# Moving five early loads from SyncE's queue to GpSimd's, behind the weights, and nine warm-up products in place of fourteen

## The chip, the cores and the metric

The kernel runs on one core of a Trainium2 chip. The metric is the device time of one execution in microseconds (us), taken as the median of several runs. Engines are named as in the profile: PE is TensorE's matmul side and PEld its weight loads, DVE is VectorE, ACT is ScalarE, POOL is GpSimd, SP is SyncE. L267 is line 267 of the kernel file before the change.

## The reference, cut to what matters

The input x has 4 sequences of 1024 rows and 256 columns, in 32-bit floats. Three residual steps follow each other:

```
def tlin(x, w, s): return einsum('bsi,oi->bso', x, w) * s      # w holds -1, 0, 1

def ffn(x):
    h = silu(tlin(x, w1, s1)) * tlin(x, w2, s2)    # 256 -> 1024
    h = gelu(tlin(h, h1, t1))                      # 1024 -> 1024
    h = gelu(tlin(h, h2, t2))                      # 1024 -> 1024
    return tlin(h, w3, s3)                         # 1024 -> 256

x = x + 0.5 * ffn(layernorm(x))
x = x + mix(layernorm(x))      # long convolution by FFT with a computed kernel, gelu, then @ W.T + b
x = x + 0.5 * ffn(layernorm(x))
```

Both feed-forward steps use the same weights. `w3s` holds s3, `wt` holds W transposed and `bias` holds b.

## The kernel before

The 4096 rows are cut into eight blocks of 512. The list of work is eight blocks of the first feed-forward step (turn "f", blocks 0 to 7), then eight of the last (turn "g"). The mixing step and the computation of its convolution kernel are Python generators that are advanced by small steps (`tick`) among the matmuls of the blocks.

For one block, `transposed` turns the normalized rows into two tiles `xt` by eight PE transposes, and `ffn` runs four layers. In the first, for each of eight groups m of 128 outputs, `linear` (L267) makes `pa` from w1 and `pb` from w2. Each takes four matmuls, since there are two groups k of inputs and each activation is held in two parts of reduced width. ACT applies the silu (L286), DVE multiplies (L287), ACT makes the first part of the result `ha` (L289) and DVE the second (L240). The layers with `h1` and `h2` take 16 matmuls for each m. The output layer (L323) uses w3, and `finish` (L332) scales by `w3s_sb`.

All weights stay on chip. They are loaded at the start in one queue, `weights_from`, which is POOL's in the form of the kernel that runs: w1 and w2 in two pieces each (256 narrow columns, then the 768 wide ones, L191 and L192), then the rows of block 1, the inputs of the convolution kernel (`k_in`), h1 and h2 in eight pieces (L201), and w3 (L202). The two halves of block 0's rows are issued by SP and ACT (L182). SP then issues small constants, `w3s_sb`, `wt_sb` and `bias_sb` (L203 to L205), and after them the rows of blocks 2 and 3 (L171, called by `load_x`). The buffers of the rows (tag "xb") are three, so that the rows of block 3 wait for block 0's buffer, which comes free when block 0 is transposed.

Ahead of block 0, PE multiplies an identity by itself N_WARM times (L880). A 32-bit product of this kind shows in the profile as two matmul instructions.

The order of the instructions on each engine is not the order of the program text. A planner orders them when the program is built, by their place in the text as a priority and by times that it expects for transfers and operations. On the chip each engine runs its own list strictly in that order: an instruction that waits holds up all behind it. Tiles of one tag share a fixed number of buffers (19 of tag "half", 15 of tag "ring", 8 PSUM banks).

`prepare` loads and normalizes the next block while the current one is computed; in the text its steps for block 2 come in the last wide layer of block 1, but the planner may place them as early as the buffer allows.

Of the kernel before, what the change touches and what calls it, by code (L numbers as in the profile page):

```python
# [17 lines left out]
P = 128  # L18
# [10 lines left out]
NA, NB = 64, 16  # L29
A0, A1 = 8, 8  # L30
JQ = J // 2
N_WARM = 14
STEPS = 2 * KH - 1
N_CHECKS = 44

# [58 lines left out]
def macaron_layers(  # L94
# [23 lines left out]
    nc = tc.nc  # L118
# [10 lines left out]
    def bank(name):  # L129
        return psum.tile([P, 512], F32, tag="ps", name=name)  # L130
# [20 lines left out]
    wt_sb = keep.tile([P, DC, D], F32, name="wt_sb")  # L151
    w3s_sb = keep.tile([P, D], F32, name="w3s_sb")
    bias_sb = keep.tile([P, D], F32, name="bias_sb")
# [11 lines left out]
    def positions(t, b, j, n=2):  # L165
        return t[b].rearrange("(p j) d -> p j d", j=J)[:, j : j + n, :]

    def load_x(t, blk, name, queue=nc.sync):
        b, g = divmod(blk, J // JT)
        xb = work.tile([P, JT, D], F32, tag="xb", name=name, bufs=3)  # L170
        queue.dma_start(xb, positions(t, b, g * JT, JT))  # L171
        return xb

    def rows(w):
        return w.rearrange("(k p) o -> p k o", p=P)


    weights_from = nc.gpsimd if split else nc.sync
# [15 lines left out]
    x_second = load_x(x, 1, "x_f1", queue=weights_from)  # L194
# [5 lines left out]
        for k in range(0, KH, 2):  # L200
            weights_from.dma_start(t[:, k : k + 2, :], rows(src)[:, k : k + 2, :])  # L201
    weights_from.dma_start(w3_sb, rows(w3))  # L202
    nc.sync.dma_start(w3s_sb, w3_s.partition_broadcast(P))  # L203
    nc.sync.dma_start(wt_sb, rows(wt))
    nc.sync.dma_start(bias_sb, bias.partition_broadcast(P))  # L205


    def norm(t, name, parts_of=1):

        stats = small.tile([P, JT, 6], F32, tag="stats", name=f"stats_{name}")  # L210
        mv = small.tile([P, JT, 2], F32, tag="mv", name=f"mv_{name}")
        rstd = small.tile([P, JT], F32, tag="rstd", name=f"rstd_{name}")
        step = JT // parts_of
        for at in range(0, JT, step):
            here = range(at, at + step)
            for i in here:
                nc.vector.bn_stats(stats[:, i, :], t[:, i, :])
            for i in here:
                nc.vector.bn_aggr(mv[:, i, :], stats[:, i, :])
            nc.scalar.activation(  # L220
                rstd[:, at : at + step], mv[:, at : at + step, 1], AF.Sqrt, bias=eps
            )
        yield
        for at in range(0, JT, step):
            nc.vector.reciprocal(rstd[:, at : at + step], rstd[:, at : at + step])
            for i in range(at, at + step):
                ts(
                    t[:, i, :],
                    t[:, i, :],
                    mv[:, i, 0:1],  # L230
                    rstd[:, i : i + 1],
                    ALU.subtract,
                    ALU.mult,
                )
        yield
# [6 lines left out]
    def transposed(xn, name, first=False):  # L242


        pts = [bank(f"pt_{name}_{k}") for k in range(DC)]
        order = [(k, i) for k in range(DC) for i in range(JT)]
        for k, i in sorted(order, key=lambda o: o[1]) if first else order:
            nc.tensor.transpose(  # L248
                pts[k][:, i * P : (i + 1) * P], xn[:, i, k * P : (k + 1) * P], ident
            )  # L250
        xt = [ring(f"xt_{name}_{k}", parts, TB, dtype=wide) for k in range(DC)]
        last = None
        if first:
            last = nc.vector.tensor_copy(xt[0][:, 0, :], pts[0])
            nc.scalar.copy(xt[1][:, 0, :], pts[1])
        for k in range(DC):
            if not first:
                nc.vector.tensor_copy(xt[k][:, 0, :], pts[k])
            if split:
                last = low_part(xt[k], pts[k])  # L260
        return (xt, last) if first else xt
# [572 lines left out]
    def prepare(turn, blk, upcoming):  # L834

        name = f"{turn}{blk}"
        if turn == "f":
            xb = x_second if blk == 1 else load_x(x, blk, f"x_{name}")
        else:
            while ("m", blk // 2) not in done:  # L840
                next(aside, None)
            xb = load_x(x2, blk, f"x_{name}")
        yield
        yield
        for _ in norm(xb, name):
            yield
            yield
        while True:
            if ("last layer", blk, turn) in done:
                upcoming.extend(transposed(xb, name))  # L850
                return
            yield
# [25 lines left out]
    warm = bank("warm")  # L878
    for i in range(N_WARM):
        nc.tensor.matmul(warm[:, 0:P], ident, ident, start=(i == 0), stop=(i == N_WARM - 1))  # L880
    for _ in norm(x_first, "f0", parts_of=2):
        pass
    xt, last_split = transposed(x_first, "f0", first=True)
    for n, (turn, blk) in enumerate(blocks):
        following = []
        steps = [prepare(*b, following) for b in blocks[n + 1 : n + 2]]

        def ahead(last=False):
            for step in steps:
                if last:  # L890
                    done.append(("last layer", *blocks[n + 1][::-1]))
                next(step, None)

        src, dst = (x, x1) if turn == "f" else (x2, out)
        with tc.issue_after(last_split.ins) if n == 0 else nullcontext():
            ffn(xt, src, dst, blk, f"{turn}{blk}", tick, ahead, n + 1 == len(blocks))
        done.append((turn, blk))
        xt = following
# [5 lines left out]
def macaron_kernel(tc: tile.TileContext, *args):  # L904
    nc = tc.nc
    with tc.tile_pool(name="flag", bufs=1) as flags:
        bad = flags.tile([1, 1], I32, name="bad")
        macaron_layers(tc, bad, *args)
        n_bad = nc.values_load(bad, min_val=0, max_val=1 << 24)
        with tc.If(n_bad > 0):  # L910
            macaron_layers(tc, None, *args)
# [65 lines left out]
```

## Time and profile before

| What | Value |
|---|---|
| Median of three runs | 1436.28 us (1435.95 to 1436.58) |
| Profiled execution: its own time | 1436.93 us |
| Profiled execution: span from first to last instruction | 1435.2 us |
| PE busy | 1420.1 us, 99% of the span |
| PEld busy | 1203.3 us, 84% |
| DVE busy | 834.3 us, 58% |
| ACT busy | 674.2 us, 47% |
| POOL busy | 79.1 us, 6% |
| Bytes moved | 85.50 MB, 60 GB/s over the span |
| Bytes moved in the first 40 us | 362 GB/s |

The page has a row for each engine with its busy time, and a strip that cuts the span into 40 slices. The transfers are dense in the first slice alone; the matmuls are dense in all but the first and last. Queue q0 in the profile is POOL's, q1 is SP's and q10 is ACT's. A timeline row gives the start, the time from the start of the first to the end of the last of a merged group, the engine and line, the operation, the output and inputs by name, the count and, in brackets, the idle time ahead of it with what ended it. Matmuls overlap, so that the distance between the starts of two, rather than the duration of one, is what PE spends on each.

### The profile page before, as it was taken

How to read it: one execution, taken by the hardware profiler on the slowest of the kernel's cores; microseconds unless marked ns; L12 is line 12 of the kernel's file. 1: busy time of each engine (PE TensorE's matmuls, PEld its weight loads, DVE VectorE, ACT ScalarE, POOL GpSimd, SP SyncE). 2: the span in 40 equal slices, each digit the busy share in tenths (PEclk: the TensorE clock that was granted, in tenths of full speed). 3: DMA queues.
4: the chain of work that ended last, by engine and by line, in shares of the span. 5: the costliest groups of instructions: out<-in, count | busy, mean ns of one | idle time of the engine just before them, and what ended most of it. 6: DMA issues, size and time to landing. Idle time of an engine off the chain costs nothing.

```text
span 1435.2 us, 18151 instructions
## 1 busy us (share of the span) xinstructions
PE 1420.1 (99%) x7102; PEld 1203.3 (84%) x7102; DVE 834.3 (58%) x1584; ACT 674.2 (47%) x1030; POOL 79.1 (6%) x77
## 2 busy tenths in 40 slices
PE   7999999999999999999999999999999999999998
PEld 6888888888888888888888888888888888888886
DVE  5786566853745587653787722966547766341422
ACT  4776458744534345334553433534344344443432
POOL 3010000100000000020000010000010000100000
PEclk9999999999999999999999999999999999999999
DMA  9110000101132130140131130231131311300000
GB/s 366 40 45 0 16 30 0 45 1 30 56 111 69 38 125 30 59 127 21 46 109 39 65 111 22 88 96 37 60 103 52 91 42 37 96 30 1 23 8 18
DMA packets 43662, 85.50 MB, mean 60 GB/s; under 512 B 4832, under 2 KB 10720, under 8 KB 43568
## 3 DMA queue, kind: packets, MB, share of 16 engines
q1 hardware_dynamic: 38864, 71.62, 15.5%
q0 software_dynamic: 4560, 12.39, 2.4%
q8 instruction: 57, 0.93, 0.3%
q14 instruction: 37, 0.30, 0.1%
q10 hardware_dynamic: 144, 0.26, 0.0%
HBM read 69.04 MB, written 15.20 MB: 59 GB/s over the span
## 4 chain that ended last, share of the span: by engine, by line
PE 97%; DVE 1%; DMA 1%; POOL 0%; issue 0%; POOLq 0%
PE p_g L267 32%; PE p_f L267 31%; PE po_g L323 4%; PE po_f L323 4%; PE pb_f L267 4%; PE pa_f L267 4%; PE pa_g L267 4%; PE pb_g L267 4%; PE pi L791 2%; PE pw L811 2%; PE pf_m L621 2%; PE pk L552 1%; DMA w_sb<-in_w_dram 1%; PE pf_k L621 0%; PE pt_g L248 0%; PE pt_f L248 0%
## 5 line engine op out<-in xcount | busy, mean ns | idle before, releaser
L267 PE MATMUL p_f<-h_f,h_sb 128*128 128x512 f32 x1024 | 239.1, 392 | 0.0
L267 PE MATMUL p_f<-ha_f,h_sb 128*128 128x512 f32 x1024 | 237.0, 391 | 0.0
L267 PE MATMUL p_g<-h_g,h_sb 128*128 128x512 f32 x1024 | 236.0, 390 | 0.0
L267 PE MATMUL p_g<-ha_g,h_sb 128*128 128x512 f32 x1024 | 235.1, 390 | 0.0
L267 PEld LDWEIGHTS p_g<-h_g,h_sb 128*128 128x128 f32 x1024 | 192.2, 188 | 39.8
L267 PEld LDWEIGHTS p_g<-ha_g,h_sb 128*128 128x128 f32 x1024 | 192.0, 188 | 39.9 <-DVE ha_g L240 0.2
L267 PEld LDWEIGHTS p_f<-ha_f,h_sb 128*128 128x128 f32 x1024 | 191.8, 188 | 39.8
L267 PEld LDWEIGHTS p_f<-h_f,h_sb 128*128 128x128 f32 x1024 | 191.3, 188 | 40.1 <-DVE h_f L240 0.3
L299 ACT ACTIVATE g_g<-p_g,sc_sb 128x512 f32<-128x512 f32 x128 | 88.1, 689 | 274.2 <-PE p_g L267 269.0
L240 DVE TENSOR_TENSOR h_g<-g_g,h_g 128x512 fp32r<-128x512 f32 x128 | 88.3, 691 | 221.1 <-ACT h_g L301 221.1
L240 DVE TENSOR_TENSOR h_f<-g_f,h_f 128x512 fp32r<-128x512 f32 x128 | 88.3, 690 | 195.5 <-ACT h_f L301 195.3
L299 ACT ACTIVATE g_f<-p_f,sc_sb 128x512 f32<-128x512 f32 x128 | 88.1, 689 | 223.2 <-PE p_f L267 216.7
L301 ACT CAST h_g<-g_g 128x512 fp32r<-128x512 f32 x128 | 79.3, 620 | 3.9
L301 ACT CAST h_f<-g_f 128x512 fp32r<-128x512 f32 x128 | 79.0, 618 | 3.3
L267 PE MATMUL pa_f<-xt_f,w_sb 128*128 128x512 f32 x256 | 71.0, 397 | 2.5 <-DMA w_sb<-in_w_dram 1.8
L267 PE MATMUL pb_f<-xt_f,w_sb 128*128 128x512 f32 x256 | 70.5, 395 | 2.8 <-DMA w_sb<-in_w_dram 2.8
L267 PE MATMUL pa_g<-xt_g,w_sb 128*128 128x512 f32 x256 | 68.6, 390 | 0.0
L267 PE MATMUL pb_g<-xt_g,w_sb 128*128 128x512 f32 x256 | 68.5, 389 | 0.0
L286 ACT ACTIVATE g_g<-pa_g,sc_sb 128x512 f32<-128x512 f32 x64 | 43.4, 688 | 52.2 <-PE pa_g L267 49.4
L286 ACT ACTIVATE g_f<-pa_f,sc_sb 128x512 f32<-128x512 f32 x64 | 43.3, 688 | 44.8 <-PE pa_f L267 43.9
L323 PE MATMUL po_f<-w_sb,h_f 128*128 128x256 f32 x512 | 64.0, 285 | 0.2 <-DVE h_f L240 0.2
L323 PE MATMUL po_g<-w_sb,h_g 128*128 128x256 f32 x512 | 63.7, 285 | 0.0
(227 smaller groups left out, 1652.8 us busy)
## 6 DMA issues: line engine op xcount, KB each, us to landing
h_sb<-in_h_dram POOLq DMA_DIRECT2D x8, 1024.0 KB, 15.2
given<-in_h_dram SPq DMA_DIRECT2D x32, 256.0 KB, 3.3
kr<-k_hat SPq DMA_DIRECT2D x20, 256.0 KB, 2.6
ki<-k_hat SPq DMA_DIRECT2D x20, 256.0 KB, 2.7
xr_f<-in_x_dram SPq DMA_DIRECT2D x16, 256.0 KB, 4.1
x<-y_f SPq DMA_DIRECT2D x16, 256.0 KB, 2.4
xm<-x SPq DMA_DIRECT2D x8, 512.0 KB, 4.6
m_m<-in_cosm_dram SPq DMA_DIRECT2D x16, 256.0 KB, 4.3
```

The source lines that it names most:

```text
L240: return tt(t[:, 1, :], src, t[:, 0, :].bitcast(F32), ALU.subtract)
L267: nc.tensor.matmul(ps, w[:, k, m * P : (m + 1) * P], acts[k][:, part, :], start=(k == 0 and part == 0), stop=(k == n - 1 and part == parts ...
L286: nc.scalar.activation(g, pa, AF.Silu, scale=sc_sb[:, 0, m : m + 1])
L299: nc.scalar.activation(g, ps, AF.Gelu, scale=sc_sb[:, layer, m : m + 1])
L301: nc.scalar.copy(t[:, 0, :], g)
L323: nc.tensor.matmul(ps[:, e * D : (e + 1) * D], ha[k][:, part, (i + e) * P : (i + e + 1) * P], w3_sb[:, k, :], start=(k == 0 and part == 0) ...
L552: nc.tensor.matmul(pk[0:NA, at + i, :, :].rearrange("p h b -> p (h b)"), a[:, i].rearrange("p a b -> p (a b)"), qd[d1 // per_tile][:, at + ...
L621: nc.tensor.matmul(ps[e][:, part, :], m[:, e, part, :], rows_of(q + JQ * e), start=True, stop=True)
L791: nc.tensor.matmul(banks[dc][e][:, q * P : (q + 1) * P], vs[q + JQ * e][:, part, dc * P : (dc + 1) * P], m[:, e, part, :], start=(part == ...
L811: nc.tensor.matmul(ps[:, e * D : (e + 1) * D], yts[dc][j // JQ][:, (j % JQ + e) * P : (j % JQ + e + 1) * P], wt_sb[:, dc, :], start=(dc == 0),
```

## The change

`w3s_sb`, `wt_sb` and `bias_sb` are loaded through the weights' queue, after w3, instead of SP's. The rows of blocks 2 and 3 (in the title's count the third and fourth, block 1 being the second and in that queue already) go through the weights' queue too; block 4 and later stay on SP's. N_WARM goes from 14 to 9. Nothing of the computation changes.

```diff
-N_WARM = 14
+N_WARM = 9
...
     weights_from.dma_start(w3_sb, rows(w3))
-    nc.sync.dma_start(w3s_sb, w3_s.partition_broadcast(P))
-    nc.sync.dma_start(wt_sb, rows(wt))
-    nc.sync.dma_start(bias_sb, bias.partition_broadcast(P))
+    weights_from.dma_start(w3s_sb, w3_s.partition_broadcast(P))
+    weights_from.dma_start(wt_sb, rows(wt))
+    weights_from.dma_start(bias_sb, bias.partition_broadcast(P))
...
         name = f"{turn}{blk}"
         if turn == "f":
-            xb = x_second if blk == 1 else load_x(x, blk, f"x_{name}")
+
+            queue = weights_from if blk < 4 else nc.sync
+            xb = x_second if blk == 1 else load_x(x, blk, f"x_{name}", queue)
```

## The prediction

> **What bounds the kernel now.** I read the page first: PE is busy for 99% of the span, and the chain that ended last is PE for 97% with a single DMA entry, `w_sb<-in_w_dram`, at 1%. The waits of PE alone name all of its idle time between first and last matmul:
>
> ```profile
> PE pb_f L267 <- DMA w_sb<-in_w_dram: 2.8, 1, 2.8
> PE warm L880 <- POOL ident masks.py:199: 2.6, 1, 2.6
> PE pa_f L267 <- DMA w_sb<-in_w_dram: 1.8, 1, 1.8
> PE pa_f L267 <- DVE xt_f L254: 0.7, 1, 0.7
> PE po_f L323 <- DVE h_f L240: 0.2, 1, 0.2
> ```
>
> Everything but the last is in the first 17 us. After that PE has no gap up to the final output stage, so a microsecond won at the head moves the end by one, unless new order creates a new gap. The timeline of PE shows the head (start, time from first start to last end, both us):
>
> ```profile
> 2.58 6.33 PE L880 MATMUL warm<-ident 128*128 128x128 f32 x28 [2.58 <-POOL ident masks.py:199]
> 8.72 1.06 PE L248 MATMUL pt_f<-ident,x_f 128*128 128x128 f32 x8
> 10.45 0.50 PE L267 MATMUL pa_f<-xt_f,w_sb 128*128 128x512 f32 x1 [0.67 <-DVE xt_f L254]
> ...
> 11.26 0.39 PE L267 MATMUL pb_f<-xt_f,w_sb 128*128 128x512 f32 x1
> 13.43 0.50 PE L267 MATMUL pa_f<-xt_f,w_sb 128*128 128x512 f32 x1 [1.79 <-DMA w_sb<-in_w_dram]
> 16.78 0.77 PE L267 MATMUL pb_f<-xt_f,w_sb 128*128 128x512 f32 x1 [2.85 <-DMA w_sb<-in_w_dram]
> ...
> 32.91 7.42 PE L267 MATMUL p_f<-ha_f,h_sb 128*128 128x512 f32 x32
> ```
>
> The first layer of block 0 is 64 matmuls (8 m, two matrices, 2 k, 2 parts). The chain of waits gives four of them 0.91 us, 0.2275 each, at full speed: 14.56 us. They take 32.91 - 10.45 = 22.46 us, so 7.9 us are lost. Two pauses for the wide columns of w1 and w2 take about 5.1 (the 4.6 of idle named above and the hand-overs). The rest is the clock. Stretches, with PE busy and the granted clock:
>
> ```profile
> 15.60:22.40 6.80, 5.62 (x13) 4.51 (x14) 2.94 (x11) 1.24 (x2) 3.77 (x5) 0.50 1.11 420
> 22.40:32.90 10.50, 10.50 (x47) 8.64 (x46) 9.56 (x21) 9.32 (x16) 0.00 (x0) 1.00 1.13 420
> ```
>
> The column after POOL is the clock: half for 6.8 us. The chain has three matmuls in 1.28 us there, 0.427 each, so 5.6 us after 16.78 hold 13 matmuls that each lose 0.2: 2.6 us. Why the weights are late shows in the DMA queues in two stretches, 5 to 10.2 us and then 13.43 to 16.78 (packets, MB, share of 16 engines):
>
> ```profile
> q1 hardware_dynamic: 612, 0.84, 57.8%
> q0 software_dynamic: 449, 0.71, 45.6%
> ```
>
> ```profile
> q0 software_dynamic: 271, 0.90, 67.8%
> q1 hardware_dynamic: 136, 0.49, 36.7%
> ```
>
> q0 is POOL's (weights), q1 is SP's: SP's later-needed tensors take about half of the engines, then a third, while PE waits for POOL's.
>
> **The Trainium skill.** "DMA: Bandwidth & Descriptors", section "Issuing engines are not separate DMA queues", says that transfers from all engines share the same 16 DMA engines and interleave; "Queues, rings and completion order" there has each engine go round-robin among the queues with work. The trace agrees: both queues above move at once and the sum is about full. "TensorE: Matmul & The Clock Gate", Part 1, has the clock at half until a free-running window of about 3.4 us was busy, and at half again after an idle one. The trace agrees: half clock lasts 6.8 us, twice 3.4. The warm-up instructions too run at half (421 ns, against 275 for the same shape at L791); the first transposes show 272 ns like all later ones, so the clock rose near 8.7, after 6.1 us of work.
>
> **The change, part by part.**
> 1. *Five transfers leave SP's queue.* w3s 128 KB, wt 256, bias 128 (issued at 2.13 to 3.08), x_f of block 2 (3.59) and of block 3 (9.8, when block 0's buffer came free), 512 each: 1.56 MB, all moved before 16.78. At the late rate of 420 GB/s that is 3.7 us; by q1's shares up to 16.78 (0.9 + 3.0 + 0.6 + 1.2 us, less 0.5 for block 0's own rows and small constants, over an engine sum of 1.1) it is 4.7. I take 4.2: w2's wide part lands near 12.6 in place of 16.75, w1's near 10, the narrow parts near 6 to 7.5 rather than 8.7 and 10.2. The issues themselves (0.43 us each on SP) were hidden.
> 2. *Five warm-ups go.* 28 instructions start 0.2115 us apart, so 18 end near 6.4, not 8.5. The last rows of block 0 are normalized at 7.5 (0.84 us from 6.66), after which one more tile is transposed. The eight transposes, at half clock about 0.21 each rather than 0.11, end near 8.4 at worst (9.78 before), and with the 0.67 us of xt cast the first wide matmul starts near 9.2 in place of 10.45: 1.2 us.
> 3. *What is then no longer waited for.* From 9.2 the first 16 matmuls need narrow weights alone; at full clock they end at 12.8, just past the 12.6 above. Both pauses (5.1) go, and with them the idle window that halved the clock (2.6). With part 2: 7.9 + 1.2 = 9.1 us, first layer over at 23.8.
> 4. *What is late next: DVE.* It runs in order, and its first block-1 statistics stood before its first result of layer one, held until x_f1 landed at 17.90; x_f1 moves with the weights to 13.7. Before, DVE needed 2.7 us from there to the first L287 (20.64), then to 35.73 for the last ha; without the cold wait and without the statistics of block 2 that stood among them (about 1.5) that stretch is about 12 us. So ha is done near 28.2, against 35.73: 7.5 us, and PE had 0.4 in hand there (it asks for the eighth ha 14 matmuls after 32.91). That caps the gain near 8.0. ACT, 9.3 busy of 10.5 us, is no tighter.
> 5. *POOL's queue.* It holds five more issues (0.6 to 0.9 each, 3.5 us), each held for an earlier transfer as its h and w3 issues already are. POOL's next work is L340 at 97.39, so the cover is 60 us or more. Total bytes are unchanged, so the five land last, where w3 did: 21.44 + 20.6 = 42. First uses: w3s at 96.6, wt at 615, bias at 618, block 2's transposes after 170. h1's last part is now near 24.5; PE asks for it 12 matmuls into layer two. SP's next wait, for x_f of block 4 at 92, is as before, and nothing else sits behind the removed ones. No cost.
> 6. *Statistics of blocks 2 and 3* must stand later on DVE. If they wait in layer two until about 41 us, the results of that layer wait with them; it uses one of eight banks per m and gives 3.63 us each, so PE has some 29 us before it runs out. No cost there. Elsewhere the planner's order may shift: no row shows it, and with PE free of gaps now I allow 1 us lost, nothing won.
>
> Sum: -8.0 us. The profiled execution took 1436.93 us (span 1435.2, 1.7 around it), so 1428.9. It lies 0.65 above the median of 1436.28; from the median the same sum gives 1428.3, inside the range.
>
> **Rivals.**
> *A, as above,* 1428.9 (1427 to 1430.3). Chance 0.60.
> *B: weights early, clock cold.* With nine warm-ups PE works from 2.58 to about 8.4, 5.8 us, then pauses for the cast. A whole window of 3.4 fits in that only if its edge falls in 2.4 of 3.4 us, 7 in 10; before it was 7.2 us and always fitted. Else the clock rises at about 12.8 to 16.2: (16 - 9.2) / 0.427 = 16 matmuls cold, 48 full, end at 26.9 for 32.91. Gain 6.0, so 1430.9. The 65% busy window from 15.6 on that didn't lift the clock speaks for it. Chance 0.26.
> *C: the move does not matter.* If q0 alone is held by its own descriptors, w2 lands at most 1 to 2 us earlier, the pause comes before the start gained by part 2, and the clock still falls. Gain 0 to 2.8; 1435.5. Against it: from 17 us on q0 alone moves 420 GB/s. Chance 0.08.
> *D: slower through DVE.* If block 2's first statistic keeps its place ahead of the first L287, DVE stands until the rows land near 41. ha is then done near 41 + 12 = 53, not 35.7: some 16 us more, 1453. It costs from the point where that landing passes the 20.6 us of the old first L287. For it: DVE already stood 6.2 us for x_f1 in this way. Against it: block 3's rows, asked for at 9.8, were put behind all eight results (35.81), so the order follows expected arrival and need. Chance 0.06.
>
> **How the numbers follow.** A and B fill 1427 to 1432 and hold 0.86; unknown slips of about 1 us widen this to 1426.8 to 1432.8. C and D are left outside. What a measurement here can tell from no change is 0.2%, 2.9 us, so A and B are faster, C is the same, D slower: 0.86, 0.08, 0.06.
>
> **What would show it.** PE's waits for `w_sb` nearly gone; first L267 near 9.2; no half clock (A) or one that starts before the first matmul (B); p_f near 24 to 25 (A) or 27 (B); q1 almost empty from 5 to 17 us; DVE's x_f1 wait ending near 13.7; the last transfers landing at about 41. A wait on w_sb past 15 us, or an L287 after 21 us, proves C or D.

## The result, and the profile after

The changed kernel takes 1430.31 us (median of six runs, 1428.99 to 1430.75), the kernel before 1436.12 (median of six, 1435.04 to 1436.58). The ratio is 0.9959 with a 95% interval of 0.9946 to 0.9972: faster, by 5.8 us. The profiled execution took 1430.35 us with a span of 1428.6; the one of before had 1436.93 and 1435.2, so this pair differs by 6.6: the profiled execution of before lay 0.8 above its median.

The timeline of PE for the head of the changed kernel, and its start of the layer with h1, which is called layer two below:

```profile
2.60 4.21 PE L882 MATMUL warm<-ident 128*128 128x128 f32 x18 [2.60 <-POOL ident masks.py:199]
6.60 1.70 PE L248 MATMUL pt_f<-ident,x_f 128*128 128x128 f32 x8
8.97 0.50 PE L267 MATMUL pa_f<-xt_f,w_sb 128*128 128x512 f32 x1 [0.67 <-DVE xt_f L254]
...
10.00 1.25 PE L267 MATMUL pa_f<-xt_f,w_sb 128*128 128x512 f32 x4
...
22.91 1.07 PE L267 MATMUL pb_f<-xt_f,w_sb 128*128 128x512 f32 x4
23.81 21.40 PE L267 MATMUL p_f<-ha_f,h_sb 128*128 128x512 f32 x92
```

Eighteen warm-up instructions end the wait for the transposes at 6.60, the first wide matmul is at 8.97 (10.45 before), and from there to 23.81 stand 64 matmuls in 14.84 us without a gap. Layer two starts 9.1 us earlier. The stretch that ran at half clock before is now at full clock (columns: the five engines, then clock, share of the DMA engines, GB/s):

```profile
15.60:22.40 6.80, 6.80 (x31) 5.63 (x31) 6.80 (x16) 5.25 (x9) 2.19 (x3) 1.00 1.13 421
```

In the DMA queues between 5 and 10.2 us, POOL's is the only one left:

```profile
q0 software_dynamic: 727, 1.77, 108.4%
```

It moved 0.71 MB in that stretch before. The landings show in POOL's own list, since a weight's issue waits until an earlier one has landed:

```profile
10.17 0.72 POOL L201 DMA_DIRECT2D h_sb<-in_h_dram  x1 [1.72 <-DMA w_sb<-in_w_dram]
12.06 0.72 POOL L201 DMA_DIRECT2D h_sb<-in_h_dram  x1 [1.17 <-DMA w_sb<-in_w_dram]
```

These are the wide parts of w1 and w2: about 10.2 and 12.0. Read in the same way, they landed near 13.7 and 16.9 before:

```profile
13.68 0.71 POOL L201 DMA_DIRECT2D h_sb<-in_h_dram  x1 [2.75 <-DMA w_sb<-in_w_dram]
16.94 0.71 POOL L201 DMA_DIRECT2D h_sb<-in_h_dram  x1 [2.54 <-DMA w_sb<-in_w_dram]
```

But PE has a new wait, which is the second line of its waits:

```profile
PE warm L882 <- POOL ident masks.py:199: 2.6, 1, 2.6
PE po_f L323 <- ACT h_f L301: 1.0, 1, 1.0
PE pa_f L267 <- DVE xt_f L254: 0.7, 1, 0.7
PE po_f L323 <- DVE h_f L240: 0.3, 1, 0.3
```

Nothing waits for `w_sb` any longer, and the output layer of block 0 now waits for ACT. ACT's timeline at that place tells why:

```profile
84.38 0.69 ACT L299 ACTIVATE g_f<-p_f,sc_sb 128x512 f32<-128x512 f32 x1
85.08 1.28 ACT L488 ACT_TABLE_LOAD   x1
86.38 0.63 ACT L488 ACTIVATE e_b<-e_b 128x512 f32<-128x512 f32 x1
86.92 0.60 ACT L301 CAST h_f<-g_f 128x512 fp32r<-128x512 f32 x1
```

The last gelu of block 0 ended at 85.07. Its cast, which PE needs, stands behind a table load and an Exp of the convolution kernel and came at 86.92. Before, the same cast stood directly behind the gelu:

```profile
91.19 0.68 ACT L299 ACTIVATE g_f<-p_f,sc_sb 128x512 f32<-128x512 f32 x1
91.90 0.62 ACT L301 CAST h_f<-g_f 128x512 fp32r<-128x512 f32 x1
```

Where the time went is read from the starts of PE's stages. This table has them for all kernels that were run; each row is one profiled execution, and the last column is the median of the timed runs. The last line is the change again, profiled and timed a second time, on the chip of the three kernels above it. The kernel before was timed again beside each group: its median was 1435.89 us for e1 to e4, 1435.53 for e5, f1, f3 and h, and 1435.51 for the last four, so that medians of different groups can be compared to about 0.6 us. The ratios below are to the timings of the same group.

| Kernel | layer two, block 0 | transposes, block 1 | block 2 | last block | median us |
|---|---|---|---|---|---|
| before | 32.91 | 90.95 | 179.70 | 1339.07 | 1436.12 |
| the change | 23.81 | 82.23 | 172.56 | 1331.95 | 1430.31 |
| e1_loads_only | 25.03 | 83.06 | 175.83 | 1335.03 | 1431.63 |
| e2_warm_only | 30.67 | 89.05 | 177.81 | 1337.05 | 1433.84 |
| e3_rows_only | 28.14 | 86.50 | 177.27 | 1336.67 | 1433.98 |
| e4_small_only | 24.57 | 84.27 | 173.02 | 1332.27 | 1430.35 |
| e5_warm4 | 25.81 | 83.85 | 174.93 | 1334.03 | 1432.41 |
| f1_no_tick | 24.41 | 83.80 | 171.40 | 1337.56 | 1434.20 |
| f3_both | 23.88 | 81.91 | 169.40 | 1336.09 | 1433.17 |
| h_small_f3 | 24.87 | 82.91 | 170.39 | 1336.81 | 1434.60 |
| g1_cast_first | 24.02 | 82.55 | 172.33 | 1331.64 | 1429.57 |
| g2_cast_norm | 24.14 | 82.17 | 171.63 | 1330.96 | 1428.77 |
| g3_small_norm | 25.20 | 83.24 | 171.99 | 1331.24 | 1428.67 |
| a_again | 23.88 | 83.27 | 173.71 | 1333.05 | 1430.45 |

The advance over before is 9.1 us at layer two, 8.7 at block 1, 7.1 at block 2, and still 7.1 at the last block. Two us were given back before 180 us, and then nothing; the spans differ by 6.6, since the last stage took 0.5 us longer in this execution. The second profile of the change gave back more in the first block (its layer two holds a wait of 1.0 us on ACT), so a single profile fixes such a part to about 1 us only. The medians are steadier: 1430.31 and 1430.45.

### The profile page after: what moved, and what is told of

It reads as the page before. It is cut to its first block, busy times and chain, and to the rows that moved or that the text cites. A ratio compares the mean times of both kernels' runs of the same rounds, so it can differ in the third digit from the quotient of the medians.

```text
span 1428.6 us, 18125 instructions
## 1 busy us (share of the span) xinstructions
PE 1416.6 (99%) x7092; PEld 1199.8 (84%) x7092; DVE 835.0 (58%) x1584; ACT 678.6 (48%) x1033; POOL 81.6 (6%) x82
## 4 chain that ended last, share of the span: by engine, by line
PE 97%; DVE 1%; ACT 1%; DMA 0%; issue 0%; POOL 0%; POOLq 0%
PE p_g L267 33%; PE p_f L267 31%; PE po_g L323 4%; PE pa_f L267 4%; PE pa_g L267 4%; PE pb_f L267 4%; PE pb_g L267 4%; PE po_f L323 4%; PE pi L791 2%; PE pw L811 2%; PE pf_m L621 2%; PE pk L552 1%; PE pf_k L621 0%; PE pt_f L248 0%; PE pt_g L248 0%; PE warm L882 0%
## 5 line engine op out<-in xcount | busy, mean ns | idle before, releaser
L323 PEld LDWEIGHTS po_f<-w_sb,h_f 128*128 128x128 f32 x512 | 62.4, 192 | 2.0 <-ACT h_f L301 1.2
```

The source lines that it names most:

```text
L323: nc.tensor.matmul(ps[:, e * D : (e + 1) * D], ha[k][:, part, (i + e) * P : (i + e + 1) * P], w3_sb[:, k, :], start=(k == 0 and part == 0) ...
```

## The experiments

My theory was that the gain is the engine share returned to w1 and w2, with the half clock that follows from their lateness, and that the missing two us come from a new order of ACT's and DVE's lists. The rivals were that the shorter warm-up makes the gain, that only part of the moved transfers matters, and that the loss has nothing to do with order.

**e1_loads_only: the transfers alone.**

```diff
-N_WARM = 9
+N_WARM = 14
```

> The five transfers moved, fourteen warm-up products as before. If the engine share given to the weights makes the gain: w2's wide part lands near 12 us, first L267 stays near 10.4, no pause, no half clock after it, layer two starts near 25.0 (23.8 with the whole change), and the time is 1431 to 1432 us. If the shorter warm-up made the gain: layer two starts near 32 and the time stays near 1436.

Measured: 1431.63 us (ratio to before 0.9973, 0.9962 to 0.9985). The first wide matmul is at 10.24, no wait on `w_sb` is left, and layer two starts at 25.03. The transfers alone make most of the head's gain, 7.9 of 9.1 us, and 4.3 us of the time. This profile also lost 4.0 us between layer two and block 2, more than the change did: the same late cast is there, and after two pauses of 0.95 and 0.63 us the clock fell to half for 3.4 us (the column before the last two):

```profile
88.00:90.40 2.40, 1.36 (x5) 1.02 (x6) 2.40 (x5) 1.63 (x2) 0.00 (x0) 0.96 0.10 38
90.50:93.90 3.40, 3.40 (x19) 3.40 (x18) 2.31 (x5) 1.05 (x2) 0.00 (x0) 0.54 0.00 0
```

**e2_warm_only: the warm-up alone.** All loads as before.

```diff
-N_WARM = 14
+N_WARM = 9
```

> Nine warm-up products alone, all transfers where they were. Engine share theory: first L267 near 9.0 rather than 10.45, but four matmuls later PE waits for w1 until 13.4 and for w2 until 16.8 as before, half clock follows; time within 1 us of 1436.1. Warm-up theory: 1434.6 or lower, the 1.5 us of the earlier start kept.

Measured: 1433.84 us (0.9985, 0.9979 to 0.9992), 2.1 us faster than the 1435.89 of before in these comparisons. The engine share theory allowed no more than 1, so this was a miss. By its number the other branch came true (1434.6 or lower), but not by the earlier start alone: the weights are as late as before, and PE shows one pause instead of two:

```profile
9.86 0.40 PE L267 MATMUL pb_f<-xt_f,w_sb 128*128 128x512 f32 x1
14.26 2.08 PE L267 MATMUL pa_f<-xt_f,w_sb 128*128 128x512 f32 x4 [4.00 <-DMA w_sb<-in_w_dram]
16.13 1.48 PE L267 MATMUL pb_f<-xt_f,w_sb 128*128 128x512 f32 x3
```

PE's lists differ. With fourteen products the planner put seven matmuls of the first part of `xt` in front (pa and pb of m = 0, 1 and 2, and pa of m = 3), of which three need wide columns. With nine it put five in front, and only the fifth needs wide columns of w1. So the remaining twelve matmuls on narrow columns fill the time until w2 lands near 16.9. The warm-up's length changes the order of work that follows it, not only its start. How much of the 2.1 us belongs to the order and how much to the earlier start was not separated.

**e3_rows_only: only the rows of blocks 2 and 3 moved, nine products.**

```diff
-    weights_from.dma_start(w3s_sb, w3_s.partition_broadcast(P))
-    weights_from.dma_start(wt_sb, rows(wt))
-    weights_from.dma_start(bias_sb, bias.partition_broadcast(P))
+    nc.sync.dma_start(w3s_sb, w3_s.partition_broadcast(P))
+    nc.sync.dma_start(wt_sb, rows(wt))
+    nc.sync.dma_start(bias_sb, bias.partition_broadcast(P))
```

> Only the rows of blocks 2 and 3 move behind the weights (1.05 of 1.56 MB); w3s, wt and bias stay first on SP; nine products. If bytes ahead of w2 decide: 0.51 MB at 420 GB/s is 1.2 us, w2's wide part lands near 13.3, PE pauses about 0.7 us, no half clock, layer two near 24.6, time near 1431. If the 1 KB packets of the three small ones cost more than their bytes (1.9 us or above): landing near 14, layer two near 25.3, time 1431.8.

Measured: 1433.98 us (0.9984, 0.9977 to 0.9991), no faster than e2, and with a wide spread, 1431.17 to 1435.15. The eight runs up to 1433.0 us show a mean granted clock of 0.998 or 0.999, and all but one of the slower thirteen 0.997. The expectation was missed. w2 landed near 14.4, as the dearer branch said, but the narrow part of w2 is late too (second line), and the clock falls:

```profile
8.73 0.50 PE L267 MATMUL pa_f<-xt_f,w_sb 128*128 128x512 f32 x1 [0.67 <-DVE xt_f L254]
10.18 0.80 PE L267 MATMUL pb_f<-xt_f,w_sb 128*128 128x512 f32 x1 [0.94 <-DMA w_sb<-in_w_dram]
```

```profile
8.70:10.10 1.40, 0.50 (x1) 0.19 (x1) 1.29 (x2) 1.28 (x1) 0.00 (x0) 0.96 1.18 407
10.10:16.80 6.70, 6.18 (x14) 4.41 (x15) 1.42 (x4) 0.69 (x1) 3.30 (x5) 0.50 1.11 420
```

This isn't the prediction's rival B, in which the clock is still cold at the first wide matmul: here it was full there and fell after the wait for a late transfer, as before the change. Layer two still starts 2.5 us earlier than in e2, but the late cast of the change is in this program too (PE waits 1.0 us for it), and at block 2 only 0.5 us is left.

**e4_small_only: only w3s, wt and bias moved, nine products.**

```diff
-            queue = weights_from if blk < 4 else nc.sync
+            queue = nc.sync
```

> Only w3s, wt and bias move behind the weights (0.51 of 1.56 MB); the rows of blocks 2 and 3 stay on SP; nine products. If bytes ahead of w2 decide: 1.05 MB more than with the whole change, 2.5 us, w2's wide part lands near 14.5, two pauses of 2 us in sum, layer two near 26, time near 1432.5. If the pause is long enough for the half clock to come back: layer two near 29 and 1435. If small packets were the whole matter: as with the whole change, 1430.3.

Measured: 1430.35 us (0.9965, 0.9952 to 0.9979), as fast as the whole change. Layer two starts at 24.57, one wait of 0.7 us for `w_sb` remains, and the wide part of w2 lands near 13.6. The late cast at the end of block 0 isn't there: in this program it stands directly behind its gelu, and block 0's output layer has its 64 matmuls in one row. Instead layer two of block 0 loses 1.7 us. PE waits there for ACT's last ha, which stands behind the table loads for block 1's normalization:

```profile
30.18 25.23 PE L267 MATMUL p_f<-ha_f,h_sb 128*128 128x512 f32 x110 [1.31 <-ACT ha_f L289]
```

So the rows of blocks 2 and 3, two thirds of the moved bytes, win 0.8 us at the head (1.0 and 1.1 in the later pairs f3 and h, g2 and g3) and bring the late cast with them, while e4 loses about as much in layer two. In the medians the sum is nothing. With nine products the three small tensors make the gain, 3.5 us over e2, and the rows alone add none. One thing speaks for the rows all the same: two of e4's five runs took 1431.7 and 1431.8 us at a mean clock of 0.996, against 0.998 and 0.999 in its other runs, and none of the eleven timed runs of the change lies under 0.998. The likely reason is half clock at the head in some runs; those runs have no profile, so it isn't shown.

**e5_warm4: four products with all transfers moved.**

```diff
-N_WARM = 9
+N_WARM = 4
```

> The whole change with four warm-up products. If a busy window ahead of the first layer is what keeps the clock full: PE works only from 2.6 to 4.3 and from about 6.3, so the first layer starts near 8.7 at half clock and the clock rises 3.4 to 6.8 us later; 1.7 to 3.4 us lost, time 1432 to 1433.5 with a wider spread. If the warm-up does not matter for the clock: 1430.2.

Measured: 1432.41 us (0.9979, 0.9971 to 0.9986), 2.1 above the change. The first wide matmuls are 0.43 us apart, against 0.23 there:

```profile
9.18 0.80 PE L267 MATMUL pa_f<-xt_f,w_sb 128*128 128x512 f32 x1 [0.57 <-DVE xt_f L254]
9.77 0.63 PE L267 MATMUL pb_f<-xt_f,w_sb 128*128 128x512 f32 x1
10.20 0.63 PE L267 MATMUL pa_f<-xt_f,w_sb 128*128 128x512 f32 x1
```

```profile
9.10:12.00 2.90, 2.82 (x7) 2.27 (x8) 1.31 (x3) 1.41 (x2) 1.00 (x2) 1.00 1.08 414
```

The clock column reads 1.00 here although the spacing says half: it holds nothing before the clock's first change, which came at 13.5 us in this profile. At the head only the spacing and the duration of the matmuls tell. Layer two starts at 25.81, two us late. The warm-up matters through the clock, as the prediction had it. Nine products were enough in all eleven profiles that have them: the first wide matmul takes 0.50 us in each, and 0.80 here.

**f1_no_tick: the step of the generator in front of block 0's output layer left to a later tick.**

```diff
         ahead(last=True)
-        tick()
+        if name != "f0":
+            tick()
```

> The whole change, and the one step of the convolution kernel's generator that the text puts between block 0's last wide layer and its output layer is left to a later tick. If the 1.2 us that the change loses between block 0 and block 1 come from ACT's list, where that step's Exp and its two table loads stand ahead of the last cast h_f: PE's 1.0 us wait on ACT h_f L301 goes, layer two of block 0 still starts near 23.8, block 2's transposes come near 171.3 (172.6 with the change), time near 1429.1. If the wait only moves elsewhere: 1430.3 as before.

Measured: 1434.20 us (0.9989, 0.9981 to 0.9998), 3.9 above the change. The wait on ACT's h_f went, as expected, and block 2 came at 171.40, though layer two started at 24.41 and had a wait of 1.0 us for ACT's ha of its own. But all later steps of the generators stand one tick later, and from block 2 to the last block PE took 1166.2 us in place of 1159.4. Part of the distance only changes sides, since block 2 comes earlier because a step's products now follow it: from block 1 to block 2 it is 87.6 us, 88.75 before. PE's waits after 200 us name 2.7 us, of which the change has only the 0.3 of `po_f`:

```profile
PE pa_f L267 <- ACT g_f L286: 1.2, 1, 1.2
PE p_f L267 <- DVE ha_f L240: 0.6, 2, 0.4
PE p_f L267 <- DVE h_f L240: 0.4, 1, 0.4
PE po_f L324 <- DVE h_f L240: 0.3, 1, 0.3
PE p_g L267 <- DVE h_g L240: 0.2, 1, 0.2
```

The whole loss lies ahead of the twelfth block of the list, whose transposes start at 977.67 (972.08 with the change); from there to the last block both take 359.9 us. Between block 2 and the twelfth, PE's idle time grows by 2.7 us and its busy time by 4.0. About 1 us of the latter is 16 matmuls that have moved there with the step. I can't account for the other 3.

**f3_both: f1, and block 1's normalization behind DVE's last ha.** `last_ha` collects the DVE instructions that make the second part of ha, and `issue_after` ties what is traced inside it behind one instruction on the same engine.

```diff
-        for _ in norm(xb, name):
+        todo = norm(xb, name)
+        while True:
+            with tc.issue_after(last_ha[KH - 1].ins) if split and name == "f1" else nullcontext():
+                if next(todo, todo) is todo:
+                    break
             yield
             yield
```

> As the kernel before it in this list, and block 1's normalization is tied behind DVE's last ha of block 0, so that neither its statistics nor its two table loads on ACT stand inside the first layer. If DVE and ACT set the 0.4 us lost in layer two: ha is done near 26 rather than 28.7, layer two takes 29.0 in place of 29.4, block 2's transposes near 170.9, time near 1428.7. If PE alone set it: no difference to the kernel before it in this list.

Measured: 1433.17 us (0.9982, 0.9975 to 0.9989). Layer two of block 0 takes 29.01 us (52.89 - 23.88), as in the kernel before the change, rather than 29.40 with the change (30.36 in f1): the normalization was what it lost to. The late part of the kernel is lost as in f1.

**h_small_f3: both edits, with the rows left on SP.** The edit of e4 on top of f3.

> The two repairs of the kernel before it in this list, but with the rows of blocks 2 and 3 left on SP and only w3s, wt and bias behind the weights. If the rows' bytes matter at all for the head: layer two starts near 24.5 (0.7 later than 23.8) and the time is near 1429.4. If they do not: as the kernel before it, 1428.7.

Measured: 1434.60 us (0.9997, 0.9989 to 1.0005). The head is as expected (24.87), and the loss after block 2 covers it. It says nothing more than f1 on the loss; for the head it agrees with e4.

**g1_cast_first: the step keeps its place, and its Exp is tied behind the cast on ACT.**

```diff
-                    nc.scalar.copy(t[:, 0, :], g)
+                    cast = nc.scalar.copy(t[:, 0, :], g)
...
         ahead(last=True)
-        tick()
+        with tc.issue_after(cast.ins) if split and name == "f0" else nullcontext():
+            tick()
```

> The whole change; the step of the generator stays at its place in the text, but on ACT its Exp is tied behind the last cast h_f of block 0. If the late cast is what loses 1.2 us at the end of block 0: PE's wait on ACT h_f L301 goes, block 1's transposes stay near 82.2, block 2's come near 171.3, and, since no later step has moved, the last block's near 1330.7 (1331.95 with the change); time near 1429.1. If any change of order starts other waits, as when the step was left to a later tick: above 1430.3.

Measured: 1429.57 us (0.9955, 0.9942 to 0.9969). The output layer's row is whole again:

```profile
83.34 8.05 PE L324 MATMUL po_f<-w_sb,h_f 128*128 128x256 f32 x64
```

From block 1's transposes to its layer two it is 23.20 us (24.31 with the change, 23.08 before), so the cast was 1.1 of the 1.2 us. But layer two of block 1 then takes 29.93 us, with a wait of 0.3 on DVE's ha, in place of 29.36 (29.01 before). Half of what was regained is lost one stage later. With a head that was 0.3 us later in this profile, that is why block 2 came at 172.33 and not at 171.3.

**g2_cast_norm: g1, and the normalization of block 1 as in f3.**

> As the kernel before it in this list, and block 1's normalization tied behind DVE's last ha of block 0. The 0.4 us of layer two in block 0 go too: last block's transposes near 1330.3, time near 1428.7. Rival: another wait takes its place, above 1429.5.

Measured: 1428.77 us (0.9952, 0.9938 to 0.9965), as expected. Layer two of block 0 takes 29.01 us, against 29.51 in g1.

**g3_small_norm: the three small tensors moved, nine products, block 1's normalization behind the last ha; rows on SP, ACT's order left to the planner.** The edits of e4 and of f3's normalization.

> Only w3s, wt and bias behind the weights, nine products, and block 1's normalization tied behind the last ha of block 0; the order of ACT at the end of block 0 is left to the planner. Layer two near 24.5 without the 1.3 us wait on ACT ha; last block's transposes near 1330.8, time near 1429.2. If the rows on SP matter more than 0.7 us: above 1430.

Measured: 1428.67 us (0.9958, 0.9945 to 0.9972); three runs lie at 1428.4 to 1428.7 and two at 1430.6 and 1431.4, these two at a mean clock of 0.997 and the three at 0.998 or 0.999. Layer two starts later (25.20), as there is a wait of 0.9 us for `w_sb`, and from there to block 2 nothing is lost: 146.79 us, as before the change.

**a_again: the change itself.**

> The change itself, unaltered, on the same chip as the three kernels before it: 1430.3, within 0.6.

Measured: 1430.45 us (0.9962, 0.9948 to 0.9975). All five runs (1429.73 to 1431.02) lie above all five of g2 (1427.95 to 1429.41) on the same chip. g2 beats the kernel before and the change, the latter by 1.7 us. g3 has the same median but two of its runs lie in the change's range, so I can't rank it.

## Why the prediction was right, and where not

It said 1428.9 us with a range of 1426.8 to 1432.8; 1430.31 was measured. The mechanism was rival A: in both profiles of the change PE waits for no weight, and the clock is full from the first wide matmul on.

- *Part 1, the transfers.* w2's wide part was to land near 12.6 and landed at 12.0; w1's near 10 and at 10.2. Right as a sum, though the seven other profiles with the same transfers moved have w2's landing anywhere from 11.7 to 12.9. But I priced the five together by bytes and shares. Split up, w2 lands 2.3 us later than with the change when the small tensors are still in front (0.51 MB, e3), and 1.5, 2.4 and 3.0 us later when the rows are (1.05 MB, e4, h and g3). That the small ones also hold back the narrow part of w2, and with it the clock, was not in the sum.
- *Part 2, the warm-up.* 1.2 us expected for the first wide matmul, 1.5 measured. That N_WARM reorders PE's list was not foreseen; e2 shows 2.1 us for the shorter warm-up and the new order together.
- *Part 3, what is no longer waited for.* 9.1 us and 23.8 for the start of layer two; both are what was measured. The reason given for the first 16 matmuls was wrong, though: the fifth in PE's list needs wide columns of w1. It ran at 10.0, just when they landed. That was luck: f1 and g1, with the same transfers, show waits of 0.3 and 0.4 us there.
- *Part 4, DVE as the cap.* ha was to be done near 28.2 and was done at 28.75 (28.06 + 0.69). The cost was to be 1.1 us and layer two lost 0.4 in this profile and 1.4 in the second. I had PE ask for the eighth ha after 14 matmuls. Where its wait for ha is listed (e4, f1, g1, a_again), it stands after 18 matmuls of layer two, so that four of the next m seem to stand in front. f3, h, g2 and g3 show that block 1's normalization is the cause: with it behind the last ha, layer two takes 29.0 us in all four. In e1 and e5 it takes no longer either, though the normalization stands where it stood; layer two starts at 25.0 and 25.8 us there.
- *Part 5, POOL's queue.* No cost, as said; the last issue is at 29.34 and POOL's next work at 91.68. The last rows land near 40, predicted 41.
- *Part 6, the order elsewhere.* This is the mis-sized term. I allowed 1 us in the range and put zero in the sum. It was 1.6: 1.2 between block 0 and block 1, shown by g1 to be ACT's late cast, and 0.35 in block 1's layer two. e1 and e3 have the late cast, and e2 and e4 do not, so it comes with the rows of blocks 2 and 3. Their normalization moves to about 47 to 58 us, into the start of block 0's last wide layer (it ended at 43 us before), and ACT's list is another one from there on; that the first brings about the second is read from the lists and not tested.

Together: 9.1 less 0.4 less 1.6 is the 7.1 of the trace, for 8.0 in the prediction; the last stage's 0.5 us makes it the 6.6 between the profiled executions. Rivals C and D did not occur: block 2's first statistic moved to 46.65, behind its rows' arrival, so DVE never stood for them. B did not occur either: in none of the eleven profiles with nine products was the clock cold at the first wide matmul, so that a chance of 0.26 looks too high. It took four products (e5) to bring it about.

What stays open: why PE is 3 us busier in f1 (the stages of f3 and h grow alike), why g1's layer two of block 1 grows by 0.6 us, and why block 0's layer two loses between 0.4 and 1.4 us in two profiles of the same kernel.

## What to carry to other kernels

Look at what else moves while the first operands are on their way: with nine products, half a megabyte of tensors that are first used at 90 and 600 us cost nearly 4 us here when it was left in front (e3), and a megabyte of later rows nothing in the median (e4), though two of the five runs with the rows in front took over 1 us more than the rest. After an edit to loads in a planned program, read the starts of each stage against before: a gain at the head shows at once, and what the new order gives back showed here two stages later, in a list of another engine. Repair such a place with a local tie between two instructions (g1, g2) rather than by shifting a step, which moved everything behind it and cost 4 us (f1).

## What the runs showed of the hardware that was not expected

The clock fell after stretches that were far from idle. In each profile its changes lie whole multiples of 3.41 us apart, so that the time can be cut into windows of that length, counted from its first change, forwards and backwards. PE's busy time in such windows (second number; transposes count, and the ends of matmuls are modelled) goes with what the clock did next. These are windows at full clock in e3 and, near its end, g2, then at half clock in e5 and f3:

```profile
6.57:9.98 3.41, 1.91 (x11) 0.94 (x9) 2.91 (x7) 1.87 (x2) 1.16 (x2) 1.00 1.17 353
1418.26:1421.67 3.41, 1.90 (x16) 1.70 (x15) 1.70 (x4) 0.00 (x0) 0.67 (x1) 1.00 0.34 121
6.69:10.10 3.41, 2.84 (x10) 1.89 (x10) 2.67 (x7) 1.44 (x2) 2.02 (x4) 1.00 1.06 365
2.38:5.79 3.41, 3.19 (x15) 3.20 (x16) 1.63 (x8) 0.57 (x3) 3.41 (x7) 1.00 1.12 304
```

After 1.91 us of work the clock fell, as it did after 0.50 (before), 0.49 (e2) and 1.82 (e1). After 1.90 it stayed full, and so it did after 1.94 (f1) and every fuller window of the fourteen profiles. At half clock, 2.84 us did not raise it and 3.19 did. So the idle window of the prediction isn't needed for the fall: in these traces the border lies near 1.9 us, 56% of a window, and for the rise between 83% and 94%. At the head of e4 one window holds 2.00 us, just above the border.

The cost of a transfer ahead of another isn't in proportion to bytes either: half as many bytes in w3s, wt and bias, whose rows are 1 KB, delayed w2 by 2.3 us, and the rows of x by 1.5 to 3.0. The first is from one profile, and landings spread by over 1 us between profiles with the same transfers.
